# The sums of a graph layer between the first layers of two pairs, in turns that serve two pairs

## Chip, cores, metric

The kernel runs on one core of a Trainium2 chip. The metric is the device time of one execution in microseconds (us); lower is better. Times of several runs are given as their median.

## What is computed

One layer of a graph network with 6250 nodes, 206250 edges sorted by destination, and rows of 256 values. Edge attributes have one polarity column and 64 raw columns. The reference, cut to what matters:

```python
h = relu(layernorm(x))
e = relu(raw @ W_e1.T + b_e1) @ W_e2.T + b_e2
edge_emb = (e * (clip(polarity, 0, 1) + 0.01)) @ W_le.T + b_le
msg = relu(h[src] + edge_emb)
aggr = segment_sum(msg, dst)                     # sum over the edges of a node
hh = (h + aggr) @ W_g1.T + b_g1
out = x + relu(layernorm(hh) * ln_g + ln_b) @ W_g2.T + b_g2
```

All is float32.

## The kernel before, in words

**Tiling.** 128 edges are a tile, four tiles a block (512 edges), two blocks a pair, and six blocks a group. A block has two units of two tiles each, so a pair has four units; there are 403 blocks, 202 pairs and 806 units. The product of W_e2 and W_le is formed once at the start (wc_s), and a row bc_s from the biases, so that an edge costs two products: the first layer (64 to 256, relu) and the edge product (256 to 256).

**Steps for an edge.**

- load_pair(q) on SyncE (SP) loads the transposed raw attributes of a pair, 64 rows for each of its two blocks, into one of four buffers (L229).
- first_layer(q), L242: for each half c of the 256 outputs and each block s of the pair, one matmul with 64 rows and 512 columns writes one PSUM tile. A pair gives four tiles. Their relu with bias empties them: three on ScalarE (L250), the fourth on VectorE (L247).
- edge_part(u), L265: four matmuls write the two tiles of a unit into one PSUM tile; VectorE adds bc_s and copies it to SBUF as msg (L272).
- gathers, L534: POOL fetches the rows hb[src] of a unit by two indirect DMAs into hg (16 buffers of a unit each).
- whole(u): two VectorE operations (L559) form msg * polarity + hg in place, and ScalarE takes the relu (L561).
- sums, that is add_pairs and add_up, L571: for each pair whose units are all whole, matmuls with a 0/1 selection matrix (32 columns for each of four tiles) add the edges of a row range into a PSUM tile pd. At the end of a group ScalarE copies pd to SBUF as ms (L579). The hg buffers come free with the sums.
- node_work(w): for every 128 nodes, matmuls spread the group sums (L657), and the node part follows (L165, L181, L191).

**PSUM.** The pool psz has six buffers of one bank each; they go round in order. First-layer tiles, edge units and the node steps all take theirs from it. The pool psd (two banks) holds the sums.

**Order.** The order is written out by hand, in one loop over the units u. forward(u) issues edge_part(u); when u % 4 == 1 it then calls turn_of(u // 4). In the first six and last six pairs each turn serves one pair. In between (by_two) every second turn serves two: first_layer(q + 2), first_layer(q + 3), the sums of the pairs that are ready (mostly two), and two raw loads, once in eight units. So a turn issues eight first-layer tiles and the sums between edge unit u and edge unit u + 1. After forward(u) the loop issues gathers, up to a limit that rises by a unit or so in each step and with the pairs summed:

```python
k = (u - TURN) % 8
gathers(4 * summed + HG - 8 + (1, 2, 3, 4, 5, 6, 6, 7)[k], last_z)
```

The first gather of such a step waits for the last edge matmul issued (last_z). Then come whole(made) for the units that have their rows, none in the step before a turn and two in the turn's own, and at most one node step (due). Each engine works through its own queue in the order of issue; waits stand in the instruction. TensorE's completions are not announced singly: where nobody waits for one, it is announced with a later matmul's.

A matmul in float32 appears in the trace as two records, so a turn for two pairs has 16 records of L242 and, for two pairs summed, 32 of L571.

Of the kernel before, what the change touches and what calls it, by code (L numbers as in the profile page):

```python
# [93 lines left out]
def gnn_kernel(ctx: ExitStack, tc: tile.TileContext, x, src_c, dst_c, dst_r, pol_c, raw_t, w_e1t, w_e2,  # L94
# [117 lines left out]
    with fast:  # L212
# [10 lines left out]
        def ps():  # L223
            return psz.tile([P, 2, D], F32, name="pz")

        def load_pair(q):
            if q < NP:
                raw[q] = ld.tile([P, 512], F32, name="raw")
                nc.sync.dma_start(out=raw[q], in_=raw_t[q])  # L229

        def first_layer(q):

            bs = [b for b in (2 * q, 2 * q + 1) if b < NB]
            if not bs:
                return
            for b in bs:
                e1[b] = e1_p.tile([P, 2, 512], F32, name="e1")
            pe = {}
            for c in range(2):
                for s, b in enumerate(bs):  # L240
                    pe[s, c] = ps().rearrange("p a b -> p (a b)")
                    nc.tensor.matmul(pe[s, c], we1_s[s * F:(s + 1) * F, c * P:(c + 1) * P],  # L242
                                     raw[q][s * F:(s + 1) * F, :], start=True, stop=True)
            for c in range(2):
                for s, b in enumerate(bs):
                    if s == c == 1:
                        nc.vector.tensor_scalar(e1[b][:, c, :], pe[s, c], be1_s[:, c:c + 1], 0.0, op0=ALU.add,  # L247
                                                op1=ALU.max)
                    else:
                        nc.scalar.activation(e1[b][:, c, :], pe[s, c], AF.Relu, bias=be1_s[:, c:c + 1])  # L250
            raw.pop(q)
# [25 lines left out]
        sums = lambda last: None  # L277

        def by_two(q):
            return FEW <= q < NP - FEW  # L280

        def turn_of(q):


            if not by_two(q):
                if q + 2 < NP:
                    first_layer(q + 2)
                sums(q == NP - 1)
                load_pair(q + 4)
            elif q % 2 == 0:  # L290
                first_layer(q + 2)
                first_layer(q + 3)
                sums(False)
                load_pair(q + 4)
                load_pair(q + 5)

        def forward(u):

            pz = edge_part(u)
            if u % 4 == TURN:  # L300
                turn_of(u // 4)
            if pz is not None:
                for i in range(2):
                    m = hg[u][:, i, :]
                    nc.vector.scalar_tensor_tensor(m, pz[:, i, :], pol_s[:, 2 * u + i:2 * u + i + 1], m, op0=ALU.mult,
                                                   op1=ALU.add)
                    nc.scalar.activation(m, m, AF.Relu)
# [212 lines left out]
        with tc.tile_pool(name="hg", bufs=HG) as hg_p, tc.tile_pool(name="ms", bufs=5) as ms_p, \  # L520
# [168 lines left out]
            sums = add_pairs  # L689
# [214 lines left out]
```

## Time and profile before

| what | before |
|---|---|
| median of 3 runs | 2613.92 us (2611.29 to 2625.64) |
| profiled execution, its own time | 2608.97 us |
| its span in the profile | 2607.1 us |
| TensorE clock granted, mean | 0.95 |
| first layers L242: busy, records | 514.7 us, 1612 |
| sums L571: busy, records | 228.5 us, 3224 |
| gathers L534: busy, mean, count | 1645.3 us, 1021 ns, 1612 |
| VectorE L559: busy, mean, count | 693.7 us, 476 ns, 1608 |

How to read the profile. It is one execution. PE is TensorE, PEld its weight loads, DVE VectorE, ACT ScalarE, POOL GpSimd, SP SyncE. In a group's line stand the source line, engine, operation, output<-inputs and shapes, the number of instructions, busy us, mean ns of one, and the engine's idle time ahead of them with what ended it. In the list of waits, "A <- B: 153.5, 151, 5.4" says that A's engine idled 153.5 us in 151 waits which B ended, the longest 5.4. "issue" is idle time without a releaser in the profile, "remote" one whose releaser it doesn't know. The timeline gives start and length in us, merged over equal neighbours, and the idle time before in brackets. The PEclk row has a digit for each fortieth of the span, in tenths of full clock.

### The profile page before, as it was taken

To read this page: it belongs to the slowest core of one execution; us is meant where nothing else is said; L and a number is where in the kernel's file an instruction comes from. 1 tells how busy PE (TensorE), PEld (TensorE's weight loads), DVE (VectorE), ACT (ScalarE), POOL (GpSimd) and SP (SyncE) were. 2 spreads that over 40 slices of the span, in tenths; PEclk is the share of its full clock that TensorE was granted. 3 is DMA by queue.
4 is the path that set the end of the run, shared out by engine and by line. 5 is a ranking of instruction groups with operands and counts; after the bars stand their busy time and mean duration, and the time that the engine had idled before them with its cause. 6 is when DMAs were issued, how large, how long until landed. Compare 5 with 4: busy or idle time off the path is not lost.

```text
span 2607.1 us, 34857 instructions
## 1 busy us (share of the span) xinstructions
PE 2395.6 (92%) x12382; PEld 1697.5 (65%) x12382; DVE 1588.1 (61%) x3473; ACT 967.9 (37%) x1701; POOL 1682.5 (65%) x1675
## 2 busy tenths in 40 slices
PE   9899989999998999999899989989999899889978
PEld 6665756676665666666567666656667666656646
DVE  6675655666665666566556556646656565656645
ACT  7333333334333333333333333433434333333323
POOL 5766666666666666666666666666666666666663
PEclk9999999999999999999899999989999999999989
DMA  8433433444434343433343334434333344343331
GB/s 296 124 115 104 121 117 108 122 124 120 121 102 125 118 121 96 133 114 111 111 130 103 109 116 123 117 102 126 114 118 116 110 122 120 101 126 113 114 105 56
DMA packets 156075, 309.17 MB, mean 119 GB/s; under 512 B 33183, under 2 KB 77944, under 8 KB 155896
## 3 DMA queue, kind: packets, MB, share of 16 engines
q0 software_dynamic: 77376, 211.39, 27.9%
q1 hardware_dynamic: 77364, 92.23, 11.3%
q10 hardware_dynamic: 1156, 3.28, 0.3%
q8 instruction: 98, 1.61, 0.2%
q14 instruction: 81, 0.66, 0.1%
HBM read 293.92 MB, written 12.85 MB: 118 GB/s over the span
## 4 chain that ended last, share of the span: by engine, by line
PE 83%; issue 6%; DVE 5%; another core or an unknown queue 2%; POOL 1%; ACT 1%; DMA 1%; POOLq 0%; ACTq 0%; DVEq 0%
PE pz L265 52%; PE pz L242 16%; PE pd L571 8%; PE pz L657 2%; DVE msg L272 2%; PE pz L191 2%; PE pz L165 1%; DVE hg L559 1%; POOL hg L534 1%; DMA hg<-hb_d,src_s 1%; ACT e L250 1%; PE pz L181 0%; DMA xt<-in_x_dram 0%; DVE st L136 0%
## 5 line engine op out<-in xcount | busy, mean ns | idle before, releaser
L534 POOL DMA_INDIRECT hg<-hb_d,src_s x1612 | 1645.3, 1021 | 867.4 <-issue 639.1
L265 PE MATMUL pz<-wc_s,e 128*128 128x256 f32 x6448 | 1523.5, 389 | 77.6 <-issue 72.7
L265 PEld LDWEIGHTS pz<-wc_s,e 128*128 128x128 f32 x6448 | 1232.5, 194 | 329.2 <-issue 149.3
L272 DVE TENSOR_TENSOR msg<-pz,bc_s 128x512 f32<-128x512 f32 x797 | 540.9, 685 | 686.8 <-PE pz L265 324.0
L561 ACT ACTIVATE hg<-hg 128x512 f32<-128x512 f32 x804 | 499.7, 629 | 1114.6 <-DVE hg L559 957.2
L559 DVE SCALAR_TENSOR_TENSOR hg<-msg,pol_s,hg 128x256 f32<-128x256 f32 x1608 | 693.7, 476 | 19.3 <-DMA hg<-hb_d,src_s 14.9
L242 PE MATMUL pz<-raw,we_s 64*128 64x512 f32 x1612 | 514.7, 653 | 87.2 <-DVE msg L272 62.4
L250 ACT ACTIVATE e<-pz,vecs 128x512 f32<-128x512 f32 x605 | 369.2, 688 | 198.6 <-PE pz L242 129.5
L242 PEld LDWEIGHTS pz<-raw,we_s 64*128 64x128 f32 x1612 | 195.8, 193 | 336.3 <-DVE msg L272 153.5
L247 DVE TENSOR_SCALAR e<-pz,vecs 128x512 f32<-128x512 f32 x201 | 150.3, 748 | 241.9 <-PE pz L242 165.1
L571 PE MATMUL pd<-hg,sel 128*32 128x256 f32 x3224 | 228.5, 414 | 13.8 <-issue 12.4
L571 PEld LDWEIGHTS pd<-hg,sel 128*32 128x32 f32 x3224 | 103.3, 118 | 179.6 <-issue 133.8
L579 ACT ACTIVATE ms<-pd 128x256 f32<-128x256 f32 x66 | 25.3, 383 | 269.4 <-remote 119.7
L657 PE MATMUL pz<-s,ms 128*128 128x128 f32 x548 | 75.0, 282 | 15.3 <-issue 15.0
L657 PEld LDWEIGHTS pz<-s,ms 128*128 128x128 f32 x548 | 72.4, 197 | 20.4 <-issue 18.0
L547 DVE TENSOR_TENSOR sel<-iota_w,rel 128x768 f32<-128x768 f32 x68 | 63.8, 939 | 0.0
L191 PE MATMUL pz<-wg_s,nT 128*128 128x256 f32 (+1 forms) x196 | 52.5, 391 | 2.4 <-issue 2.4
L165 PE MATMUL pz<-wg_s,hT 128*128 128x256 f32 (+1 forms) x196 | 51.2, 381 | 1.1 <-issue 1.1
L377 POOL TENSOR_TENSOR hb<-xt,rows_b 128x256 f32<-128x256 f32 (+1 forms) x49 | 34.2, 729 | 24.1 <-ACT xt L373 17.2
L191 PEld LDWEIGHTS pz<-wg_s,nT 128*128 128x128 f32 (+1 forms) x196 | 38.6, 198 | 9.3 <-issue 3.7
L165 PEld LDWEIGHTS pz<-wg_s,hT 128*128 128x128 f32 (+1 forms) x196 | 36.9, 189 | 9.8 <-issue 4.3
L636 DVE TENSOR_TENSOR hT<-hT,stb 128x256 f32<-128x256 f32 (+1 forms) x98 | 40.7, 415 | 0.0
(89 smaller groups left out, 383.5 us busy)
## 6 DMA issues: line engine op xcount, KB each, us to landing
raw<-in_raw_t_dram SPq DMA_DIRECT2D x202, 256.0 KB
hg<-hb_d,src_s POOLq DMA_INDIRECT x1612
stb<-st_d SPq DMA_DIRECT2D x49, 128.0 KB
hb_d<-hb SPq DMA_DIRECT2D x12, 512.0 KB
xt<-in_x_dram SPq DMA_DIRECT2D x48, 128.0 KB
hT<-in_x_t_dram SPq DMA_DIRECT2D x48, 128.0 KB
out_dram<-ot SPq DMA_DIRECT2D x48, 128.0 KB
xt<-in_x_dram SPq DMA_DIRECT2D x11, 512.0 KB
```

The source lines that it names most:

```text
L165: nc.tensor.matmul(ph[:n, 0, :], aT[:, c, :n], wg1_s[:, c, :], start=c == 0 and not bias_by_pe, stop=c == 1)
L191: nc.tensor.matmul(po[:n, 0, :], nT[:, c, :n], wg2_s[:, c, :], start=c == 0, stop=c == 1)
L242: nc.tensor.matmul(pe[s, c], we1_s[s * F:(s + 1) * F, c * P:(c + 1) * P], raw[q][s * F:(s + 1) * F, :], start=True, stop=True)
L247: nc.vector.tensor_scalar(e1[b][:, c, :], pe[s, c], be1_s[:, c:c + 1], 0.0, op0=ALU.add, op1=ALU.max)
L250: nc.scalar.activation(e1[b][:, c, :], pe[s, c], AF.Relu, bias=be1_s[:, c:c + 1])
L265: last_z = nc.tensor.matmul(pz[:, i, :], e1[b][:, c, k:k + P], wc_s[:, c, :], start=c == 0, stop=c == 1)
L272: nc.vector.tensor_add(msg[u], pz, bc_s)
L534: g = nc.gpsimd.indirect_dma_start(out=hg[u][:, i, :], out_offset=None, in_=hb_d, in_offset=bass.IndirectOffsetOnAxis(ap=src_s[:, 2 * u + ...
L559: nc.vector.scalar_tensor_tensor(hg[u][:, i, :], m[:, i, :], pol_s[:, 2 * u + i:2 * u + i + 1], hg[u][:, i, :], op0=ALU.mult, op1=ALU.add)
L561: nc.scalar.activation(hg[u], hg[u], AF.Relu)
L571: nc.tensor.matmul(pd[g][j * W:(j + 1) * W, :], sel[g][:, k * S + j, :], m[:, j % 2, :], start=k == 0, stop=b == blocks_of(g)[-1])
L657: nc.tensor.matmul(pa[:, c, :n], ms[g][:, c * P:(c + 1) * P], box["sel2"][i][:, :n], start=i == 0, stop=i == len(gs) - 1)
```

## The change

In the branch for two pairs the call of the sums moves from behind both first layers to between them.

```diff
@@ turn_of(q)
             elif q % 2 == 0:
                 first_layer(q + 2)
+                sums(False)
                 first_layer(q + 3)
-                sums(False)
                 load_pair(q + 4)
                 load_pair(q + 5)
```

Nothing is added or taken away. On TensorE such a turn is then four first-layer tiles, the sums, four first-layer tiles. On ScalarE the copy of a finished group (L579) comes before the second pair's three relu copies instead of behind them. VectorE, POOL and SP have the same instructions in the same order. The sums' waits for the relus (L561), which the waits of the second pair's tiles used to cover, stand in the sums themselves.

## The prediction

> **What bounds the kernel now.** I read the page's first two parts, then the chain that ended last, the groups, the list of waits, and last the TensorE timeline turn by turn.
>
> ```profile
> span 2607.1 us, 34857 instructions
> PE 2395.6 (92%) x12382; PEld 1697.5 (65%) x12382; DVE 1588.1 (61%) x3473; ACT 967.9 (37%) x1701; POOL 1682.5 (65%) x1675
> ...
> PEclk9999999999999999999899999989999999999989
> ...
> PE pz L265 52%; PE pz L242 16%; PE pd L571 8%; PE pz L657 2%; DVE msg L272 2%; PE pz L191 2%; PE pz L165 1%; DVE hg L559 1%; POOL hg L534 1%; DMA hg<-hb_d,src_s 1%; ACT e L250 1%; PE pz L181 0%; DMA xt<-in_x_dram 0%; DVE st L136 0%
> ```
>
> TensorE is busy for 92% of the span, and three lines of it, the edge products (L265), the first layers (L242) and the sums (L571), hold 76% of the chain. The change moves the last two against each other, so the question is what TensorE loses around them. The groups price the pieces, the waits say who is late:
>
> ```profile
> L242 PE MATMUL pz<-raw,we_s 64*128 64x512 f32 x1612 | 514.7, 653 | 87.2 <-DVE msg L272 62.4
> L250 ACT ACTIVATE e<-pz,vecs 128x512 f32<-128x512 f32 x605 | 369.2, 688 | 198.6 <-PE pz L242 129.5
> L571 PE MATMUL pd<-hg,sel 128*32 128x256 f32 x3224 | 228.5, 414 | 13.8 <-issue 12.4
> ```
>
> ```profile
> DVE msg L272 <- PE pz L265: 324.0, 164, 22.7
> DVE msg L272 <- remote: 167.7, 36, 9.1
> ...
> PEld pz L242 <- DVE msg L272: 153.5, 151, 5.4
> ...
> ACT ms L579 <- remote: 119.7, 17, 20.0
> ...
> PE pz L242 <- DVE msg L272: 62.4, 65, 4.6
> ```
>
> The first layers wait for VectorE's message copies (L272): eight first-layer tiles follow each other, and only six PSUM buffers turn round, so tiles 5 and 6 need the buffers of the last two edge units. Two turns on the TensorE timeline, one with that wait and one without:
>
> ```profile
> 488.63 3.14 PE L242 MATMUL pz<-raw,we_s 64*128 64x512 f32 x8
> 492.90 2.58 PE L242 MATMUL pz<-raw,we_s 64*128 64x512 f32 x8 [1.13 <-DVE msg L272]
> 495.41 1.93 PE L571 MATMUL pd<-hg,sel 128*32 128x256 f32 x32
> 497.28 5.45 PE L265 MATMUL pz<-wc_s,e 128*128 128x256 f32 x24
> ```
>
> ```profile
> 2016.66 3.70 PE L242 MATMUL pz<-raw,we_s 64*128 64x512 f32 x16
> 2020.29 1.93 PE L571 MATMUL pd<-hg,sel 128*32 128x256 f32 x32
> 2022.15 0.48 PE L265 MATMUL pz<-wc_s,e 128*128 128x256 f32 x1
> 2022.84 0.59 PE L265 MATMUL pz<-wc_s,e 128*128 128x256 f32 x2 [0.20 <-issue]
> 2024.26 1.02 PE L265 MATMUL pz<-wc_s,e 128*128 128x256 f32 x4 [0.83 <-issue]
> ```
>
> Without a wait the eight tiles take 3.63 us and the sums 1.86. At 488.63 the same tiles take 6.78, and the sums, which need none of those PSUM buffers, stand behind the wait. The second turn has its gaps after the sums: TensorE's completions reach VectorE and ScalarE late. In the timeline around such places the release comes 1.3 to 2 us after a run of back-to-back gathers (L534) ends; here the gathers run from 2006.6 to 2028.1, and the copy of the sums (L579) starts at 2030.10, 8 us after the sums. Why the completions come late I can't tell from the trace.
>
> **What the Trainium skill says.** "TensorEngine Tiling (Array Packing)", Tiling Modes: a switch between tiling modes drains TensorE. The trace agrees, at a small price: between pairs of first-layer records the step is 0.43 us, but 0.53 at the first and 0.52 at the last, so about 0.2 for one stretch in 64-row mode. The same page, Performance Considerations: tiled matmuls shift the limit to emptying PSUM. The trace agrees: two tiles take 0.86 us, one ScalarE copy about 0.69. "TensorE: Matmul & The Clock Gate", Part 1: idle TensorE falls to half clock. The mean clock here is 0.95, and 21 of the 89 regular turns run partly at half rate. The same page says that ScalarE and VectorE keep strict queue order; I use it below, and no wait in this trace contradicts it.
>
> **The change part by part.** I took the 89 turns with 16 first-layer and 32 sum records from the timeline, measured in each the time lost from tile 5 on to the sums, and subtracted: the sums can cover at most 1.86 us of it, and a second stretch in 64-row mode costs 0.2.
>
> - 22 turns lose nothing there: 22 x -0.2 = -4 us.
> - 46 turns at full clock lose 72.7 us in all (16 of them 1.9 to 3 us each). Each capped at 1.86, less 0.2: 54 us gained.
> - 21 turns with half clock lose 106.8 us, half rate included; almost all reach the cap: 35 us gained.
>
> Sum 85 us. Where the stall goes: if tiles 5 and 6 come after the sums, the message copies have 1.86 us more, and tiles 7 and 8 wait for ScalarE's copies of tiles 1 and 2, some 1.2 to 2.5 us after the turn starts: hidden. Next late is tile 5's own copy.
>
> What the move adds:
>
> - Waits of the sums on ScalarE. In the built program the number of sum matmuls that wait rises from 21 to 387, since the later tiles' waits used to imply them. In the trace of before the relu (L561) that each needs ends before the turn starts in all but three turns; the sums would start 1.82 us in, and the latest needed relu in a four-block turn comes at 1.35. Cost 0 (0.6 us once, in a turn with 48 sum records).
> - Queue order. VectorE's, POOL's and SP's orders are unchanged. VectorE's copy of tile 8 (L247, 0.75 us) finds its tile 1.9 us later, and behind it wait four L559 (1.66 us) and the next L272. VectorE is at 61%; six units' buffers, 10 us, lie between that L272 and its user. Cost 0 on the path; with that cover gone, 0.7 us a turn.
> - On ScalarE the copy of the sums (L579, 66 of them, 0.38 us) now stands before the second pair's three copies (L250). If the sums' completion is late, these are held, and the third edge unit after the turn needs tile 5's buffer, 3.46 us after tile 8. In the trace of before the message copy after the sums came over 3.1 us late in 21 turns, by 44 us beyond that in all. In these TensorE crawls anyway (the gaps at 2022), so between 0 and 44; I take half, 22 us lost.
> - Slots for gathers come free with the sums, some 1.8 us earlier, so POOL's second unit of the turn may start earlier, and a pause in its gathers shrinks (matching the built program's waits to the trace, 51 pauses on L571, 111 us). As late completions end at pauses, part of the gain comes back as lateness elsewhere. POOL runs 16 gathers a turn at about 1.3 us, 21 of 25 us. Bounds: 0, and the whole gain. I take 25 us.
> - The turn's two raw loads on SP wait for the pair whose buffer they take; the second is up to 1.9 us later, and used a turn (25 us) afterwards. Cost 0; without that lead, a load that is late by 1.9.
>
> Net 85 - 22 - 25 = 38 us. The profiled execution took 2608.97 us (span 2607.1 and 1.9 around it), 5 us under the median 2613.92. Taken off the median: 2576 us, 1.5% faster.
>
> **The rivals.** (1) The cover works fully, and with shorter gaps the half-clock stretches thin out. For it: the 21 half-clock turns lose 5 us each. Against: they also idle for other reasons. It gives 85 us and some 15 of the clock: 2514. (2) It is washed out: the time is set by gathers plus their pauses, and the saved wait reappears after the sums. For it: turns without a wait in the first layers often lose as much right after (next two edge units up to 10.1 us in place of 3.56). It gives about 2612. (3) Slower: the second pair's completions get stuck behind the sums', ScalarE's L579 holds L250, and the third edge unit waits for tile 5's buffer. Place: the 21 turns above and those which join them; price: the saved wait returns, 18 us for the mode switches and 22 or more for held buffers stay: 2654, or 2632 where a sixth of the gain survives with it. It decides once completions after the sums come over 3.1 us late in about half of the turns. (4) That the change doesn't do what it says is excluded: the built order has four tiles, sums, four tiles in the turns for two pairs.
>
> **How the numbers follow.** Main case 0.50 at 2576 (own range 2545 to 2600); rival 1 0.12; rival 2 0.16; rival 3 0.22. Faster by over 0.5% (13 us, about what a measurement of this kernel can tell) 0.62, within 0.16, slower 0.22. The range runs from rival 1 to the middle of rival 3: 2514 to 2642, leaving out about 0.05 below and 0.12 above.
>
> **What would show it.** Right: the wait of L242 on L272 (216 us on both rows) falls under 80; on the timeline the sums stand after four tiles, without a gap ahead of the second four. Mode switch: an unstalled turn takes 5.7 us from the first tile to the next edge unit in place of 5.50. Wrong: waits of L265 on L250 copies two units after the turn, L250 waiting behind L579, or the gaps marked "issue" growing. The prediction fails if the completions of tiles 5 to 8 come as late as those of the sums do now, or if POOL's idle time shrinks while TensorE's doesn't.

## The result and the profile after

The changed kernel takes 2633.19 us (median of 11 runs, 2618.83 to 2651.26), the kernel before beside it 2611.29 us (11 runs). The ratio is 1.0089, 95% interval 1.0064 to 1.0114: slower by 0.9%, where 1.5% faster was forecast. The profiled execution took 2632.49 us.

The page of the changed kernel first: the span and the busy times, then the chain that ended last by line.

```profile
span 2630.5 us, 34857 instructions
PE 2390.1 (91%) x12382; PEld 1681.7 (64%) x12382; DVE 1578.0 (60%) x3473; ACT 980.3 (37%) x1701; POOL 1699.9 (65%) x1675
...
PE pz L265 50%; PE pz L242 15%; PE pd L571 8%; PE pz L657 2%; DVE hg L559 2%; PE pz L191 2%; ACT e L250 2%; PE pz L165 2%; DVE msg L272 1%; DVE st L136 0%; PE pz L181 0%; ACT xt L373 0%; ACT hg L561 0%; DMA we_s<-in_w_e_dram 0%
```

TensorE is busy for about as long as before (2395.6), the span is 23 us longer: the loss is new idle time. On the chain L272 has given way to L250 (2%). The groups say where the idle time went:

```profile
L265 PE MATMUL pz<-wc_s,e 128*128 128x256 f32 x6448 | 1532.9, 392 | 122.5 <-ACT e L250 76.9
...
L247 DVE TENSOR_SCALAR e<-pz,vecs 128x512 f32<-128x512 f32 x201 | 150.4, 748 | 766.7 <-remote 400.1
...
L250 ACT ACTIVATE e<-pz,vecs 128x512 f32<-128x512 f32 x605 | 378.2, 685 | 498.8 <-remote 249.4
L242 PE MATMUL pz<-raw,we_s 64*128 64x512 f32 x1612 | 477.7, 647 | 21.4 <-issue 15.1
```

Two of these groups in the kernel before:

```profile
L265 PE MATMUL pz<-wc_s,e 128*128 128x256 f32 x6448 | 1523.5, 389 | 77.6 <-issue 72.7
...
L247 DVE TENSOR_SCALAR e<-pz,vecs 128x512 f32<-128x512 f32 x201 | 150.3, 748 | 241.9 <-PE pz L242 165.1
```

The first layers hardly wait any more (87.2 us of idle time before, 21.4 now). The edge products do, for ScalarE's copies. VectorE's idle time ahead of L247 has gone from 241.9 to 766.7 us, ScalarE's ahead of L250 from 198.6 to 498.8. The list of waits of the changed kernel gives the causes:

```profile
DVE e L247 <- remote: 400.1, 60, 17.9
ACT e L250 <- remote: 249.4, 58, 14.7
...
DVE e L247 <- PE pz L265: 160.4, 21, 17.5
...
PEld pz L265 <- ACT e L250: 110.4, 56, 7.5
...
PE pz L265 <- ACT e L250: 76.9, 30, 7.3
...
PEld pz L242 <- DVE msg L272: 26.9, 44, 2.9
```

The last row was 153.5 us before. Of the two rows of L265 behind L250, the kernel before has only one:

```profile
PEld pz L265 <- ACT e L250: 1.6, 3, 0.8
```

One turn shows how they come about. TensorE, ScalarE, VectorE and POOL on the timeline of the changed kernel:

```profile
1370.26 1.99 PE L242 MATMUL pz<-raw,we_s 64*128 64x512 f32 x8
1372.18 1.93 PE L571 MATMUL pd<-hg,sel 128*32 128x256 f32 x32
1374.05 1.99 PE L242 MATMUL pz<-raw,we_s 64*128 64x512 f32 x8
1375.96 3.72 PE L265 MATMUL pz<-wc_s,e 128*128 128x256 f32 x16
1384.74 2.93 PE L657 MATMUL pz<-s,ms 128*128 128x128 f32 x12 [5.06 <-ACT e L250]
```

```profile
1375.36 0.38 ACT L579 ACTIVATE ms<-pd 128x256 f32<-128x256 f32 x1 [1.36 <-PE pz L242]
1384.01 1.84 ACT L250 ACTIVATE e<-pz,vecs 128x512 f32<-128x512 f32 x3 [8.26 <-remote]
```

```profile
1384.07 0.75 DVE L247 TENSOR_SCALAR e<-pz,vecs 128x512 f32<-128x512 f32 x1 [10.67 <-remote]
```

```profile
1379.80 0.95 POOL L534 DMA_INDIRECT hg<-hb_d,src_s  x1 [0.30 <-issue]
1381.05 0.95 POOL L534 DMA_INDIRECT hg<-hb_d,src_s  x1 [0.30 <-issue]
1384.87 1.17 POOL L534 DMA_INDIRECT hg<-hb_d,src_s  x1 [2.87 <-ACT e L250]
```

The turn itself runs as intended: four tiles, sums, four tiles, 5.70 us without a gap. Tiles 5 to 8 are done by 1376.0. ScalarE and VectorE, idle, learn of it at 1384, 2 us after POOL's run of gathers ended at 1382.0. Meanwhile TensorE has done two edge units, and then stands for 5.06 us before the next work that needs a buffer (here a node step, L657).

The trace also holds the updates of TensorE's semaphore, by which it announces its completions. In experiments 5 and 6 below, with plain loads, each comes within 0.06 us of the end of its matmul. In this turn there is one at 1375.34 and none until 1381.81, though four announcing matmuls end in between: so it is the announcement that comes late, not the engine that waits for it. Stretches in which an announcement is over 3 us late number 114 in the kernel before and 134 in the changed one (512 and 694 us in all), 102 to 157 in the other kernels of experiments 1 to 12 that gather, and none with plain loads or in experiments 13 to 18. So they are there in every order of the turn, and their number doesn't follow the time (145 in the fastest of these kernels, 111 in one that is 2.5% slower than the kernel before); what differs is which completions fall into them. Of the 134, 68 end in a pause of POOL (over 0.6 us, or within 0.2 us behind one) and 66 inside a run of gathers, so a pause is not the only thing that ends them. It can also be their result, since gathers wait for TensorE.

To count by tile, I matched each wait of the built program to the instruction that it waits for in the trace, and took as lateness the time from the end of that instruction to the start of an idle consumer. VectorE's copy of tile 8 is over 1 us late in 17 of 93 cases in the kernel before (5 over 3 us), and in 71 of 95 in the changed one (60 over 3 us). The table gives what TensorE loses around the 94 turns with eight tiles and sums (steps between records less their length in an unstalled turn), and this count. A loss is booked at the work that started late. The 17 and 34 us with plain loads, where nothing waits for long, come from the reckoning and stand in the other columns too, about as large. Columns from different chips differ in level; shapes are what to compare. (Held and split are experiments 3, 11 and 10, plain loads 5 and 6.)

| us lost at | before | after | held to tile 5 | held to tile 8 | split | plain loads, before | plain loads, after |
|---|---|---|---|---|---|---|---|
| tiles 1 to 4 | 37 | 23 | 107 | 145 | 29 | -1 | -1 |
| tiles 5 to 8 | 173 | 80 | 59 | 71 | 83 | 2 | 14 |
| sums | 71 | 120 | 93 | 113 | 118 | 17 | 17 |
| edge unit 1 behind | 88 | 104 | 58 | 55 | 95 | 34 | 38 |
| edge unit 2 | 61 | 139 | 54 | 32 | 69 | 0 | 0 |
| edge unit 3 | 17 | 19 | 42 | 7 | 36 | 0 | 0 |
| all, with units 4 to 8 | 480 | 500 | 430 | 437 | 443 | 52 | 69 |
| tile 8 late by over 1 us | 17 of 93 | 71 of 95 | 57 of 95 | 46 of 95 | 60 of 91 | 0 of 95 | 0 of 95 |

After against before: tiles 1 to 8 gain 107 us, the sums and edge units 1 and 2 lose 143, the rest gains 16. The sum, 20 us lost, is near the difference of the two spans, 23 us.

### The profile page after: what moved, and what is told of

It is laid out like the page before. It is cut to its first block, busy times and chain, and to the rows that moved or that the text cites. A ratio compares the mean times of both kernels' runs of the same rounds, so it can differ in the third digit from the quotient of the medians.

```text
span 2630.5 us, 34857 instructions
## 1 busy us (share of the span) xinstructions
PE 2390.1 (91%) x12382; PEld 1681.7 (64%) x12382; DVE 1578.0 (60%) x3473; ACT 980.3 (37%) x1701; POOL 1699.9 (65%) x1675
## 4 chain that ended last, share of the span: by engine, by line
PE 80%; another core or an unknown queue 6%; issue 6%; DVE 5%; ACT 3%; DMA 0%; ACTq 0%; DVEq 0%; POOLq 0%
PE pz L265 50%; PE pz L242 15%; PE pd L571 8%; PE pz L657 2%; DVE hg L559 2%; PE pz L191 2%; ACT e L250 2%; PE pz L165 2%; DVE msg L272 1%; DVE st L136 0%; PE pz L181 0%; ACT xt L373 0%; ACT hg L561 0%; DMA we_s<-in_w_e_dram 0%
## 5 line engine op out<-in xcount | busy, mean ns | idle before, releaser
L534 POOL DMA_INDIRECT hg<-hb_d,src_s x1612 | 1662.6, 1031 | 873.7 <-issue 512.5
L265 PE MATMUL pz<-wc_s,e 128*128 128x256 f32 x6448 | 1532.9, 392 | 122.5 <-ACT e L250 76.9
L265 PEld LDWEIGHTS pz<-wc_s,e 128*128 128x128 f32 x6448 | 1243.0, 196 | 414.7 <-issue 128.7
L561 ACT ACTIVATE hg<-hg 128x512 f32<-128x512 f32 x804 | 505.7, 631 | 852.3 <-DVE hg L559 723.1
L559 DVE SCALAR_TENSOR_TENSOR hg<-msg,pol_s,hg 128x256 f32<-128x256 f32 x1608 | 692.1, 476 | 7.9 <-DMA hg<-hb_d,src_s 6.7
L272 DVE TENSOR_TENSOR msg<-pz,bc_s 128x512 f32<-128x512 f32 x797 | 540.5, 683 | 226.9 <-PE pz L265 121.1
L247 DVE TENSOR_SCALAR e<-pz,vecs 128x512 f32<-128x512 f32 x201 | 150.4, 748 | 766.7 <-remote 400.1
L250 ACT ACTIVATE e<-pz,vecs 128x512 f32<-128x512 f32 x605 | 378.2, 685 | 498.8 <-remote 249.4
L242 PE MATMUL pz<-raw,we_s 64*128 64x512 f32 x1612 | 477.7, 647 | 21.4 <-issue 15.1
L242 PEld LDWEIGHTS pz<-raw,we_s 64*128 64x128 f32 x1612 | 163.1, 193 | 241.1 <-issue 181.3
L571 PE MATMUL pd<-hg,sel 128*32 128x256 f32 x3224 | 247.4, 389 | 54.4 <-issue 51.4
L571 PEld LDWEIGHTS pd<-hg,sel 128*32 128x32 f32 x3224 | 107.0, 110 | 216.6 <-issue 163.0
L579 ACT ACTIVATE ms<-pd 128x256 f32<-128x256 f32 x66 | 25.4, 385 | 251.4 <-remote 125.4
L657 PE MATMUL pz<-s,ms 128*128 128x128 f32 x548 | 74.1, 286 | 10.9 <-ACT e L250 6.3
L657 PEld LDWEIGHTS pz<-s,ms 128*128 128x128 f32 x548 | 72.8, 202 | 14.8 <-ACT e L250 7.3
```

The lines of the kernel that those rows point to most:

```text
L265: last_z = nc.tensor.matmul(pz[:, i, :], e1[b][:, c, k:k + P], wc_s[:, c, :], start=c == 0, stop=c == 1)
L272: nc.vector.tensor_add(msg[u], pz, bc_s)
L534: g = nc.gpsimd.indirect_dma_start(out=hg[u][:, i, :], out_offset=None, in_=hb_d, in_offset=bass.IndirectOffsetOnAxis(ap=src_s[:, 2 * u + ...
L559: nc.vector.scalar_tensor_tensor(hg[u][:, i, :], m[:, i, :], pol_s[:, 2 * u + i:2 * u + i + 1], hg[u][:, i, :], op0=ALU.mult, op1=ALU.add)
L561: nc.scalar.activation(hg[u], hg[u], AF.Relu)
L571: nc.tensor.matmul(pd[g][j * W:(j + 1) * W, :], sel[g][:, k * S + j, :], m[:, j % 2, :], start=k == 0, stop=b == blocks_of(g)[-1])
```

## The experiments

**Theories.** *Late completions:* the sums free slots for gathers, POOL then runs gathers back to back, and what TensorE does behind the sums is announced late. In the kernel before that was edge units, now it is tiles 5 to 8. Its first part, which the expectations call *early gathers*, is that gathers start sooner because slots come free sooner. *Missing cover:* tiles 5 to 8 stand directly ahead of the edge units that need their buffers. Rivals: the *held copies* (L579 ahead of L250), the *switch price* (94 more stretches in 64-row mode), *VectorE's queue* (a late L247 holds L559 and L272), *POOL's pauses* (what counts is how long the gathers stand). Every ratio is to the kernel before, measured beside it on the same chip, with a 95% interval. Experiments 1 to 12 ran on chips where the kernel before takes 2570 to 2610 us.

**1. L579 behind the second pair's copies.**

```diff
                 first_layer(q + 2)
                 sums(False)
                 first_layer(q + 3)
+                while held:
+                    held.popleft()()
```

The list held takes the copy L579 in add_up.

> The changed kernel, with the copy of the finished group's sums (L579 of before) put on ScalarE behind the second pair's three copies (L250) again, as it stood in the kernel before; all else as changed. Theory of the missing cover (tiles 5 to 8 now stand directly ahead of the next edge units, so their copies, which come late, hold the buffers): the time stays at that of the changed kernel within 5 us, 1.007 to 1.011 of before, and the edge units keep about 80 us of waits on L250. Theory of the held copies (L579 ahead of them holds L250): 20 us or more come back, 1.002 or less of before, and the waits on L250 fall by half.

Measured: 1.0116 (1.0074 to 1.0158). Nothing came back. L579 stands in nobody's way, and the waits ahead of L250 have not shrunk:

```profile
ACT e L250 <- remote: 293.5, 44, 18.3
...
ACT e L250 <- PE pz L265: 180.0, 32, 14.2
ACT e L250 <- PE pz L242: 177.8, 81, 18.5
...
PEld pz L265 <- ACT e L250: 102.9, 53, 5.5
```

The held copies fall.

**2. Sums ahead of both first layers.**

```diff
+                sums(False)
                 first_layer(q + 2)
                 first_layer(q + 3)
-                sums(False)
```

> The turn as sums, then both first layers: eight tiles in one stretch, so no second change of tiling mode, and nothing between tile 8 and the next edge unit, as in the changed kernel. Theory of the missing cover: slower than before like the changed kernel, 1.006 to 1.02, with the lost time in the two edge units after the turn. Theory of the switch price (94 turns x 0.2 us make up the 20 us): without the second stretch the time falls to before's or under it, 0.990 to 1.002. Theory of the early gathers: the slots come free still earlier than in the changed kernel, so at least as slow as that, 1.009 or more.

Measured: 1.0907 (1.0857 to 1.0957), far beyond the ranges of the first two theories. "1.009 or more", of the early gathers, holds in its words, but foresaw nothing of this size. There is one stretch in 64-row mode only, so what is lost here isn't the switch price. The lateness has moved with the sums: tile 4 is over 1 us late in 64 of 94 turns, tile 8 in 16 of 91. The waits of the kernel:

```profile
PEld pz L242 <- ACT e L250: 296.5, 75, 16.0
...
PE pz L242 <- ACT e L250: 234.7, 50, 15.0
```

Here the tiles wait for the late copies of their own turn (tile 7 takes tile 1's buffer), TensorE loses 401 us at tiles 5 to 8, and no other work lies between.

**3. Gathers held to tile 5.**

```diff
                     k = (u - TURN) % 8
+                    if k == 0:
+                        gathers(4 * summed + HG - 8, last_z)
+                        gathers(4 * summed + HG - 7, tile1)
```

Here tile1 is the matmul of tile 5, and the second unit's first gather waits for it.

> The changed kernel, with the turn's second unit of gathers waiting for the first tile of the second pair, so that it starts no earlier against the turn's end than in the kernel before. Theory of the early gathers (slots freed 1.8 us sooner shrink POOL's pauses and make completions late): at least half of the loss returns, 0.998 to 1.004 of before. Theory of the missing cover, and that of the switch price: unchanged, 1.007 to 1.011.

Measured: 0.9976 (0.9952 to 0.9999). The loss of 0.9% is gone, by a wait on POOL alone; tile 8 is late in 57 turns in place of 71, and edge unit 2 loses 54 us. (The edit moves lines by 3 or 4: L250 and L253 are L247 and L250.)

```profile
PEld pz L268 <- ACT e L253: 77.5, 53, 6.8
...
PE pz L268 <- ACT e L253: 44.9, 26, 6.4
```

187 us on the two rows have become 122. (The changed kernel itself did not run beside this one; its 1.0089 is from another comparison.)

**4. A second stretch in 64-row mode alone.**

```diff
                     pe[s, c] = ps().rearrange("p a b -> p (a b)")
+                    if switch and s == c == 0:
+                        nc.tensor.matmul(pe[s, c][:, :16], ident, ident[:, :16], start=True, stop=True)
```

> The kernel before, with one small matmul in 128-row mode (16 columns, in a PSUM tile that the next first-layer tile overwrites) between the first layers of the two pairs, so that the 64-row stretch is cut in two as in the changed kernel and the sums stay behind. Theory of the switch price: slower by about as much as the changed kernel, 1.006 to 1.011 of before (94 turns x 0.2 us = 19 us, or a little more with the small matmul). Theory of the missing cover: most of the switch lies inside waits for buffers, 1.000 to 1.004.

Measured: 1.0046 (1.0023 to 1.0069), 12 us. Between the two expectations: the switch is a real cost, 6 to 18 us by the interval, where the whole loss is 23.

**5 and 6. Plain loads in place of the gathers, both orders.**

```diff
-                        g = nc.gpsimd.indirect_dma_start(out=hg[u][:, i, :], out_offset=None, in_=hb_d, ...)
+                        a = (2 * u + i) % 48 * P
+                        g = nc.sync.dma_start(out=hg[u][:, i, :], in_=hb_d[a:a + P, :])
```

> The kernel before, with every indirect gather of POOL replaced by a plain load of 128 successive rows of hb, same size and same waits, issued by SyncE: the rows fetched are other ones, so the sums are of other data. It is the base for the next run, 0.93 to 1.0 of before. Theory of the late completions (they come late while POOL's gathers run back to back): the losses after the sums nearly vanish, and the waits of the first layers on L272 are what remains.

> The changed kernel with the same plain loads in place of the gathers (other rows, so sums of other data). Theory of the late completions: without gathers the copies of tiles 5 to 8 come in time, the cover by the sums is a gain, and this is faster than the plain-load kernel before by 20 us or more. Theory that the place of tiles 5 to 8 alone costs (their copies have no cover, whoever else runs): it is slower than the plain-load kernel before, by about 20 us.

Measured: 2156.41 us (0.8263, 0.8225 to 0.8301) and 2174.03 us (0.833, 0.8292 to 0.8368). The base is far faster than I had expected. The first-layer group of each page, of the order before and then of the changed order:

```profile
span 2154.9 us, 34655 instructions
PE 2142.3 (99%) x12382; PEld 1627.8 (76%) x12382; DVE 1592.6 (74%) x3473; ACT 968.8 (45%) x1701; POOL 37.3 (2%) x63
...
L242 PE MATMUL pz<-raw,we_s 64*128 64x512 f32 x1612 | 377.9, 603 | 0.0
```

```profile
span 2172.2 us, 34655 instructions
PE 2161.3 (100%) x12382; PEld 1605.5 (74%) x12382; DVE 1581.5 (73%) x3473; ACT 985.0 (45%) x1701; POOL 37.3 (2%) x63
...
L242 PE MATMUL pz<-raw,we_s 64*128 64x512 f32 x1612 | 401.8, 616 | 0.0
```

No idle engine starts a tile's copy over 1 us late: the mean is 0.2 us on VectorE, 0.75 on ScalarE, whose copies queue behind each other. And the first-layer matmuls don't stand for L272 in either order: with six buffers and eight tiles there is no such stall when completions come in time. So there is nothing to cover, and the move costs 17.6 us, 0.19 us a turn, which is the switch price as the prediction read it from the trace. The edit swaps the issuing engine, the queue and the addresses of the loads at once; which of these takes the lateness away isn't shown. "Faster by 20 us or more" was wrong, and "slower by about 20" right by another cause than it names: the table finds the loss at tiles 5 to 8 and edge unit 1, with no edge unit waiting long for L250 (0.8 us at most).

**7 and 8. The turn's second unit of gathers a step later, both orders.**

```diff
-gathers(4 * summed + HG - 8 + (1, 2, 3, 4, 5, 6, 6, 7)[k], last_z)
+gathers(4 * summed + HG - 8 + (0, 2, 3, 4, 5, 6, 6, 7)[k], last_z)
```

> The kernel before, with the limit for gathers in the turn's own step lower by one, so that the turn's second unit of gathers is issued one step later, behind the next edge unit. Theory of the early gathers (in the changed kernel they start too soon): in the kernel before they don't, so nothing is gained, 0.998 to 1.006. Theory of the pause (any pause in POOL's gathers at the turn lets the completions through): faster, 0.995 or less.

> The changed kernel with the same lower limit in the turn's own step. Theory of the early gathers, and that of the pause: the loss returns as with the gathers held to the second pair's first tile, 0.993 to 1.001 of before. Theory that only the wait on the second pair's tile did it: still 1.005 or more.

Measured: 1.08 (1.0756 to 1.0844) and 1.0538 (1.0487 to 1.059). A pause as such doesn't help, and an edge unit later is much too late. A likely reason is that the gathers themselves come too late: POOL's pauses (on L265 and L571, from the matched trace) are 610 us in the first against 359 in the kernel before, and 512 in the second against 369 in the changed kernel. Both expectations for the first were wrong; of those for the second, that of the early gathers and the pause was wrong, and the "1.005 or more" holds in its words only, since it gave no such size. The gathers leave room for a small shift only.

**9. Tile 8 copied by ScalarE.**

```diff
-                    if s == c == 1:
+                    if s == c == 1 and not (by_two(q - 3) and q % 2 == 1):
                         nc.vector.tensor_scalar(e1[b][:, c, :], pe[s, c], be1_s[:, c:c + 1], 0.0, ...)
```

> The changed kernel, with the copy of tile 8 (the second pair's L247) on ScalarE instead of VectorE, so that VectorE's queue has no late tile ahead of its L559 and L272. Theory of VectorE's queue (the late L247 at its head holds the messages): half of the loss or more returns, 1.003 of before or less. Theory of the late completions (whatever stands behind the sums is announced late, because the sums free slots and POOL's gathers start a run): which engine copies makes no difference, 1.005 to 1.012, and ScalarE's idle time takes over what VectorE had.

Measured: 1.0082 (1.0055 to 1.0108). VectorE's queue falls. ScalarE's idle time ahead of L250 did not grow by what VectorE had, though (444.6 us, 498.8 in the changed kernel); that part of the expectation was wrong.

**10. Sums split: one pair's between, the others' behind.**

```diff
                 first_layer(q + 2)
-                sums(False)
+                sums(False, 1)
                 first_layer(q + 3)
+                sums(False)
```

> The turn as first layers, sums of one pair, first layers, sums of the other pairs. Theory of the late completions: the first pair's sums free the slot that the turn's second unit of gathers waits for, as in the changed kernel, so tiles 5 to 8 are still late and it is as slow as that, 1.006 to 1.012 of before. Theory of the missing cover: half of the sums stand between tile 8 and the next edge unit again, so about half of the loss returns, 1.001 to 1.006.

Measured: 0.995 (0.9927 to 0.9973). Tiles 5 to 8 are late as foreseen (tile 8 in 60 of 91 turns), and yet all of the loss is gone and a little more; neither theory gave that. Edge unit 2 loses 69 us in place of 139. The waits of L265 for L250 in the split:

```profile
PEld pz L265 <- ACT e L250: 14.6, 26, 0.8
...
PE pz L265 <- ACT e L250: 0.6, 2, 0.3
```

The matmul's own row has gone from 76.9 us to 0.6. With half of the sums, some 0.93 us, behind tile 8 these waits are nearly gone, so a late copy alone does not decide: it must also meet work that needs its buffer at once.

**11. Gathers held to tile 8.** As 3, with the matmul of tile 8 for that of tile 5.

> The changed kernel with the turn's second unit of gathers held to the second pair's last tile instead of its first, some 0.9 us later. Theory of the late completions: VectorE's copy of tile 8 is over 1 us late in fewer than 25 of the 95 turns (71 in the changed kernel, 57 with the gathers held to the first tile), and the time is 0.985 to 1.000 of before. Theory that POOL's pauses are the price (with gathers one step later both kernels had over 100 us more pauses and were 5 to 8% slower): the lateness falls but the longer pause costs more, 1.003 to 1.03.

Measured: 0.9938 (0.9909 to 0.9966), the lowest of all; tile 8 is late in 46 turns, more than foreseen, but in 18 by over 3 us (60 in the changed kernel). POOL's pauses fell to 339 us: those on L265 went from 307 to 164. Of the first theory the time held and the count failed; the second failed. (L268 and L253 are L265 and L250.)

```profile
POOL hg L538 <- PE pz L243: 123.4, 68, 7.1
...
PEld pz L268 <- ACT e L253: 41.4, 38, 3.3
```

**12. One more slot for gathers in the kernel before.**

```diff
-        with tc.tile_pool(name="hg", bufs=HG) as hg_p, ...
+        with tc.tile_pool(name="hg", bufs=HG + 1) as hg_p, ...
```

> The kernel before with one more buffer for gathered rows (17) and the same limits, so that the turn's second unit of gathers no longer waits for the sums of its own turn. Theory of the late completions: the pauses on the sums (51, 111 us) vanish, POOL runs through the turn, tiles 5 to 8 are announced late as in the changed kernel (tile 8 over 1 us late in 40 turns or more, 17 before), and the additional buffer gains nothing, 0.998 to 1.015 of before. Theory that POOL's pauses are the price: a hundred us of pauses less make it faster, 0.96 to 0.985.

Measured: 1.0246 (1.0206 to 1.0285). A buffer more makes it 2.5% slower, more than either theory gave. The pauses on the sums vanish (51 to 5), and come back on L265 (248 to 380 us); tile 8 is late in 37 of 93 turns, more than twice as often (40 or more were foreseen), and TensorE loses 155 us in the sums (71 before) and 126 in edge unit 1 (88). The order on TensorE is that of the kernel before: so an earlier start of the gathers is enough to make the kernel slower.

**13 to 18. On chips without late completions.** The split together with gathers held to tile 8, and the changed kernel with 17 slots, were to show whether lateness and cover are two costs. Both went to a chip where the kernel before takes 2204.37 us. They and two more kernels, run again, came to another such chip (2205.55 us).

> Both cures in one: first layers, sums of one pair, first layers, sums of the other pairs (alone 0.995 of before), and the turn's second unit of gathers held to the last first-layer tile (alone 0.9938). If lateness and missing cover are two costs, the gains add up: 0.978 to 0.990. If they are one cost (a late copy hurts only where no other work covers it), the second cure finds little left: 0.991 to 0.998. If the pauses of POOL are what then counts: 0.998 or more.

> The changed kernel with one more buffer for gathered rows (17), so that the turn's second unit of gathers waits for no sums of its own turn; the same edit made the kernel before 2.5% slower. Theory of the early gathers: they start still earlier against tiles 5 to 8, tile 8 is over 1 us late in 60 turns or more, and the time is 1.012 to 1.035 of before. Theory that in the changed kernel the sums come early enough for the slots not to matter: 1.005 to 1.011.

> The changed kernel once more, on whichever chip this is. Where completions come late (the kernel before near 2600 us): 1.006 to 1.012 of before, as in the first comparison. Where they don't (near 2204 us): the late copies and the waits that the move was to cover are both absent, and the second stretch in 64-row mode is what remains, at most 1.008 (17.6 us, as with the plain loads), and if POOL's own gathers set the time there, 1.000.

> Sums split and gathers held, as in the run before on a chip without late completions. Where completions come late: 0.978 to 0.990 if lateness and missing cover are two costs, 0.991 to 0.998 if they are one, 0.998 or more if POOL's pauses are what then counts. Where they don't: 0.999 to 1.002 again.

> Sums split, gathers as they are. Where completions come late: 0.993 to 0.998 as before. Where they don't: 0.999 to 1.008, like the changed kernel.

> The changed kernel with one more buffer for gathered rows. Where completions come late: 1.012 to 1.035 by the theory of the early gathers, tile 8 over 1 us late in 60 turns or more; 1.005 to 1.011 if slots don't matter there. Where they don't: 0.999 to 1.002 again.

| kernel | ratio to before | interval |
|---|---|---|
| split and held, first chip | 1.0 | 0.9991 to 1.0009 |
| changed, 17 slots, first chip | 0.9999 | 0.9988 to 1.001 |
| changed, second chip | 1.0 | 0.999 to 1.001 |
| split and held, second chip | 1.0003 | 0.9994 to 1.0013 |
| split, second chip | 1.0008 | 1.0 to 1.0017 |
| changed, 17 slots, second chip | 0.9996 | 0.9986 to 1.0006 |

The page of the changed kernel there:

```profile
span 2205.8 us, 34857 instructions
PE 2183.0 (99%) x12382; PEld 1615.1 (73%) x12382; DVE 1596.6 (72%) x3473; ACT 978.9 (44%) x1701; POOL 1653.8 (75%) x1675
...
L534 POOL DMA_INDIRECT hg<-hb_d,src_s x1612 | 1616.5, 1003 | 498.0 <-issue 353.6
...
L242 PE MATMUL pz<-raw,we_s 64*128 64x512 f32 x1612 | 415.7, 619 | 5.8 <-DVE msg L272 5.8
```

The same gathers run nearly without pause (1616.5 us and the 498.0 ahead of them, mostly the 0.3 us that stand ahead of each, make 2114 of 2206), and of 95 copies of tile 8 none is late. Neither the waits that the move was to cover nor those it brought are there in size, and its time is that of the kernel before. The medians of all six runs lie between 2204.76 and 2206.82 us, whatever their order on TensorE and their slots, and the switch price of 17.6 us doesn't show either. That fits with gathers that set the pace there. It isn't proved: TensorE is busy for 99% of this span too, and I have no trace of the kernel before on such a chip. The expectations of 15 to 18 for a chip without lateness held; those of 13 and 14 named no such case. So gathers are needed for the lateness (there is none with plain loads), but long runs of them don't suffice: something comes in that differs from one chip, or one time, to another.

## Why the prediction was wrong

- **The gain, 85 us: right in size at its place, wrong in kind.** The wait of L242 on L272 fell to 31.1 us on both rows (26.9 and 4.2), under the 80 named, and tiles 1 to 8 gained 107 us. But I had read it as a structural wait, eight tiles on six buffers. With plain loads the same order shows no such wait. So nearly all of it was lateness, and lateness covered at one place was paid at the next.
- **Where the stall goes, "next late is tile 5's own copy": this step failed.** I took tiles 5 to 8 to be announced as they were before, and looked for the next wait within the turn. Behind the sums their announcement is late (tile 8: 17 cases to 71), and with nothing between tile 8 and the edge units the copies are waited for: edge unit 2 lost 78 us more, edge unit 1 16, and the sums 49, so 143 us against the 107 gained. The condition under which the prediction fails, completions of tiles 5 to 8 as late as those of the sums, was named in it and came true; I gave it no share of the sum beyond two terms of 22 and 25 us.
- **Gathers, 25 us lost within "0 and the whole gain": near in size, its reason half right.** The gathers' start does matter: holding them to tile 5 took the time from 1.0089 to 0.9976 of before, 29 us of 2570, holding them to tile 8 to 0.9938, 39 us, both taken between separate comparisons. But "late completions end at pauses" is so for 68 of 134 long stretches only, and the held kernels have no fewer of these (148 and 145, 722 and 676 us in all). By this count the holding changed the place of the lateness, not its amount.
- **L579 ahead of L250, 22 us: wrong.** Moving it back brought nothing (1.0116). What L250 waits for is the tile's announcement.
- **Mode switch, 0.2 us a turn: right.** 5.70 us in an unstalled turn as named; 12 us with the small matmul, 17.6 us with plain loads, against some 18 in the forecast. The Trainium skill ("TensorEngine Tiling (Array Packing)", Tiling Modes) says only that a switch drains TensorE; these runs agree and price it.
- **Waits of the sums on the relus, queue order on VectorE: 0, right.** No wait of L571 on the relu L561 is in the list of the changed kernel's waits, and tile 8 on ScalarE brought nothing back (1.0082).
- **The rivals.** The third named the end, 2632 to 2654, and the held buffers behind the turn, though by L579. That the measured 2633 lies so near its 2632 is luck: a sixth of the 85 us is 14, which gives 2640; 2632 is the price of the switches alone, 18 us over the median. Its deciding point, over 3.1 us late in half of the turns, was passed (tile 8: 60 of 95 over 3 us). The chance of 0.22 was low for a case whose cause the prediction itself could not explain.

What remains open: why completions are announced late while gathers run, and on some chips or at some times only; what ends such a stretch when POOL doesn't pause; and whether the earlier gathers and the missing cover are two costs or one. Each cure alone takes more than the whole loss away, but the runs of both together fell on chips without lateness.

## What to carry over

Before a wait is covered, ask whether it is one of structure or of announcement. If an idle engine starts late after its input is done, moving work ahead of the waiting instruction can move the lateness to whatever now stands there, as it did here; so put work there whose result nobody needs soon. When an edit frees a buffer earlier, follow what its owner starts with it: here a shift of the gathers' start (0.9938) was worth as much as a better order on TensorE (0.995). Of the versions tried, the changed order with the turn's second unit of gathers held to tile 8 had the lowest ratio where completions come late (0.9938; the split's 0.995 can't be told from it). Where they don't, no version that ran there gained or lost anything.

## What the runs showed of the hardware

- The completion of tile 8 came up to 14 us late in the changed kernel (done at 362.6, copied at 376.9 us), and none was over 1 us late on the two chips of experiments 13 to 18, with the same gathers; the kernel before takes 2570 to 2611 us where the first is seen, 2204 to 2206 on those two.
- TensorE's semaphore was updated within 0.06 us of the matmul's end with plain loads. With gathers on the slower chips it was over 3 us late in 114 stretches of the kernel before and 134 of the changed one, each time with no update in between.
- With plain loads of the same size and the same waits in place of the gathers, the kernel before took 453 us less (2156.41 against 2609.63).
- One more buffer for gathered rows made the kernel before 2.5% slower (1.0246, experiment 12).
